# Three buffers instead of two for the gathered rows of a graph layer's first edge pass

## The chip, the core and the metric

The kernel runs on one core of a Trainium2 chip. The metric is device time in microseconds for one execution of the whole program, as the median of several runs.

## The reference, cut to what matters

The reference is four graph layers, each followed by a feed-forward layer, on 3125 nodes of 256 features and 50000 edges. The edges are sorted by destination. The change lies in the first graph layer, which sends two rounds of messages over the edges. Each edge has one of 16 relation types with a block-diagonal matrix of its own, and a weight:

```python
def _rel_graph_conv_bdd(x, src, dst, etype, norm, w, loop_w, bias):
    xs = x[src].reshape(e, nb, -1)
    we = w[etype]
    msg = jnp.einsum('ebi,ebio->ebo', xs, we)
    msg = msg.reshape(e, -1) * norm
    agg = jax.ops.segment_sum(msg, dst, num_segments=n)
    return agg + bias + x @ loop_w

h = jax.nn.relu(_rel_graph_conv_bdd(x, src, dst, etype, norm, w1, loop_w1, b1))
return _rel_graph_conv_bdd(h, src, dst, etype, norm, w2, loop_w2, b2)
```

Everything that follows (feed-forward layers with experts, attention over edges, a top-k graph layer) is not touched by the change.

## The kernel before, in words

Nodes are cut into 25 tiles of 125. The edges that end in one tile are laid out as T = 17 chunks of 128, one edge per partition. Before the first pass, the product of every node with every relation's matrix is written to a table in HBM, `rel_tab[0]`, with a row of 256 floats for each pair of node and relation.

A pass over the edges then goes through the tiles. For tile t, `front` makes two things. `one_hot` (L1255, on DVE) writes 17 masks `s` of 128 x 125: row by edge, the edge's weight in the column of its destination. `gathered` (L1233, on POOL) issues 17 indirect DMAs, one for each chunk, each of which fetches the 128 table rows that the chunk's edges name into a slice of the tile `g`. `edge_sums` (L1262, on PE) multiplies mask and rows chunk by chunk and adds all 17 products into one PSUM bank. Since the operands are 32-bit, each of the 17 products shows as two matmul records, with two weight loads.

`skewed` sets the order: `front(t)` is issued before `back(t - 1)`, so that a tile's gathers are issued one tile ahead of its sums. `g` and `s` come from pools with rotating buffers: with two of them, the gathers of tile t + 1 have to wait until the sums of tile t - 1 have read the buffer. POOL executes its gathers in order.

In the first pass, `back1` follows the sums of a tile with a good deal of other work: it adds `own_tab`'s row block and applies Relu (L1586, L1587), transposes the result (L1205), forms its products with all 16 relations for the second pass (`relation_rows`, L1495, evicted by DVE and ACT at L1046 and L1048), and writes them to `rel_tab[1]`, some 2 MB per tile, from SP's queue (L1055, L1056). It multiplies by the second loop matrix (L1594) and adds to `x` (L1596). Between these, `count` advances a generator that prepares counting tables for later layers (masks `kh` and `lh` on DVE at L1381 and L1383, matmuls at L1397 and L1411, evictions at L1401, L1414 and L1416). This is one instruction stream per engine, in the order in which it is written.

The second pass uses the same `front` with `layer` = 1 and reads `rel_tab[1]`, so it can gather only after the first pass has written all of it. Its sums are added to `x` at L1619; experts of the first feed-forward layer are woven into it.

Of the kernel before, what the change touches and what calls it, by code (L numbers as in the profile page):

```python
# [1022 lines left out]
def fast(ctx: ExitStack, tc: tile.TileContext, a: dict, out: bass.AP):  # L1023
# [14 lines left out]
    def bank():  # L1038
        return psum.tile([128, 512], F32, tag="ps", name="ps")
# [13 lines left out]
    def dma_rows(dst, src):  # L1053

        nc.sync.dma_start(dst[0:112], src[0:112])  # L1055
        return nc.sync.dma_start(dst[112:P], src[112:P])  # L1056
# [100 lines left out]
    def load_w(src, dst):  # L1157

        nc.sync.dma_start(dst, src.rearrange("(k p) m -> p k m", p=128))
        return dst  # L1160

    def load_row(src):

        n = src.shape[0]
        r = row_pool.tile([128, D], F32, tag="row", name="row")
        nc.sync.dma_start(r[:, :n], src.partition_broadcast(128))
        return r[:, :n]
# [9 lines left out]
    def over(row, n=NT):  # L1177
        return row[:P, None, :].to_broadcast([P, n, row.shape[1]])
# [21 lines left out]
    def transpose_tiles(src, dst, n):  # L1200

        for k in range(2):
            ps = bank()
            for i in range(n):
                nc.tensor.transpose(ps[:, i * P:(i + 1) * P], src[:, i, k * 128:(k + 1) * 128],  # L1205
                                    ident[:P, :P])
            evict(dst[:, k, :], ps[:, :n * P])
# [29 lines left out]
    def gathered(pool, table, idx, t, wide=0):  # L1237

        w = table.shape[1]
        g = pool.tile([128, T, max(w, wide)], F32, tag="g", name="g")  # L1240
        for k in range(T):
            gather(g[:, k, 0:w], table, idx, t * T + k)
        return g

    def one_hot(pool, t, w=None):


        s = pool.tile([128, T, P], F32, tag="s", name="s")
        for k in range(T):
            c = t * T + k  # L1250
            if w is None:
                nc.vector.tensor_scalar(s[:, k, :], iota, dst_l[:, c:c + 1], None,
                                        op0=ALU.is_equal)
            else:
                nc.vector.tensor_scalar(s[:, k, :], iota, dst_l[:, c:c + 1], w[:, c:c + 1],  # L1255
                                        op0=ALU.is_equal, op1=ALU.mult)
        return s

    def edge_sums(ps, s, g, w, start=True, stop=True):

        for k in range(T):
            nc.tensor.matmul(ps[:P, :w], s[:, k, :], g[:, k, 0:w],  # L1262
                             start=(start and k == 0), stop=(stop and k == T - 1))

    def skewed(front, back):

        held = front(0)
        for t in range(1, NT):
            nxt = front(t)
            back(t - 1, held)  # L1270
            held = nxt
        back(NT - 1, held)
# [187 lines left out]
    def relation_weights(pool, w):  # L1460


        mask = pool.tile([128, 128], F32, name="mask")
        half = pool.tile([128, 128], I32, name="half")
        halfp = pool.tile([128, 1], I32, name="halfp")
        halff = pool.tile([128, 1], F32, name="halff")
        nc.gpsimd.iota(half, pattern=[[1, 128]], base=0, channel_multiplier=0)
        nc.gpsimd.iota(halfp, pattern=[[0, 1]], base=0, channel_multiplier=1)
        nc.vector.tensor_scalar(half, half, 1, None, op0=ALU.arith_shift_right)
        nc.vector.tensor_scalar(halfp, halfp, 1, None, op0=ALU.arith_shift_right)  # L1470
        nc.vector.tensor_copy(halff, halfp)
        nc.vector.tensor_copy(mask, half)
        nc.vector.tensor_scalar(mask, mask, halff, None, op0=ALU.is_equal)
        wc = pool.tile([128, 2, R, 2], F32, tag="wc", name="wc")
        for k in range(2):
            nc.sync.dma_start(wc[:, k, :, :],
                              w[:, 64 * k:64 * (k + 1), :, :].rearrange("r b i o -> (b i) r o"))
        wbd = pool.tile([128, 2, R * 128], F32, tag="wbd", name="wbd")
        for k in range(2):
            nc.vector.tensor_mul(  # L1480
                wbd[:, k, :].rearrange("p (r j o) -> p r j o", r=R, o=2),
                wc[:, k, :, None, :].to_broadcast([128, R, 64, 2]),
                mask.rearrange("p (j o) -> p j o", o=2)[:, None, :, :]
                .to_broadcast([128, R, 64, 2]))
        return wbd
# [58 lines left out]
    def l0_gnn():  # L1544
        with ExitStack() as st:
            keys = st.enter_context(tc.tile_pool(name="l0", bufs=1)).tile(
                [128, 2, NT * NB], F32, name="keys")
            nc.sync.dma_start(keys, key_tab)
            cp = st.enter_context(tc.tile_pool(name="cnt0", bufs=2))
            work = counting(cp, keys)  # L1550
            ffn = None

            def count(n):
                for _ in range(n):
                    next(work, None)

            def front(layer, pools):
                hp = pools.enter_context(tc.tile_pool(name=f"hot{layer}", bufs=2))
                gp = pools.enter_context(tc.tile_pool(name=f"g{layer}", bufs=2))

                def f(t):
                    s = one_hot(hp, t, wgt)
                    g = gathered(gp, rel_tab[layer], rel_x, t)
                    return s, g
                return f

            with ExitStack() as s1:
                xp = s1.enter_context(tc.tile_pool(name="l0x", bufs=1))
                yp = s1.enter_context(tc.tile_pool(name="rely", bufs=2))
                tp = s1.enter_context(tc.tile_pool(name="h0", bufs=2))  # L1570
                ffn = SoftExperts(xp)
                loop = load_w(a["L0_gnn_loop_w2"], xp.tile([128, 2, D], F32, name="loop"))
                b2 = load_row(a["L0_gnn_b2"])
                wbd = relation_weights(xp, a["L0_gnn_w2"])
                for t0, n in GROUPS:
                    dma_rows(x[:, t0:t0 + n, :], x_view[:, t0:t0 + n, :])
                    nc.vector.tensor_add(x[:, t0:t0 + n, :], x[:, t0:t0 + n, :], over(b2, n))

                def back1(t, sg):
                    s, g = sg  # L1580
                    own = tp.tile([P, D], F32, tag="own", name="own")
                    dma_rows(own, own_tab[t * P:(t + 1) * P, :])
                    ps = bank()
                    edge_sums(ps, s, g, D)
                    h = tp.tile([P, 1, D], F32, tag="h", name="h")
                    nc.vector.tensor_add(h[:, 0, :], ps[:P, :D], own)  # L1586
                    nc.scalar.activation(h[:, 0, :], h[:, 0, :], AF.Relu)  # L1587
                    count(3)
                    ht = tp.tile([128, 2, P], F32, tag="ht", name="ht")
                    transpose_tiles(h, ht, 1)  # L1590
                    relation_rows(yp, rel_tab[1], ht, wbd, t, 0)
                    ps = bank()
                    for k in range(2):
                        nc.tensor.matmul(ps[:P, :D], ht[:, k, :], loop[:, k, :],  # L1594
                                         start=(k == 0), stop=(k == 1))
                    nc.vector.tensor_add(x[:, t, :], x[:, t, :], ps[:P, :D])  # L1596
                    count(4)

                skewed(front(0, s1), back1)

            ffn.load(st)
            queue = []

            groups = {1: (0, 2), 4: (2, 3)}
            groups.update({t0 + 3: (t0, 4) for t0 in range(5, NT, 4)})

            def feed(n):
                for _ in range(n):
                    while queue and next(queue[0], queue) is queue:
                        queue.pop(0)  # L1610

            def back2(t, sg):
                s, g = sg

                parts = 7 if t < 4 else 3
                count(parts)
                ps = bank()
                edge_sums(ps, s, g, D)
                nc.vector.tensor_add(x[:, t, :], x[:, t, :], ps[:P, :D])  # L1619
                count(parts)  # L1620
                feed(3)
                if t in groups:
                    queue.append(ffn.parts(*groups[t]))

            skewed(front(1, st), back2)
            count(1000)
            feed(1000)
# [1222 lines left out]
```

## Time and profile before

| what | value |
|---|---|
| median of 3 runs | 5268.94 us (5267.66 to 5290.92) |
| profiled execution | 5201.46 us, span 5199.8 us |
| PE busy over the span | 4044.8 us (78%) |
| DVE, ACT, POOL busy | 2545.4, 1434.1, 1522.9 us |
| first gather of the first pass | 299.15 us |
| last sum of the first pass | ends at 1035.18 us |
| first gather of the second pass | 1051.45 us |
| mean granted TensorE clock | 0.867 |

The first pass takes some 740 us, a seventh of the span; the change touches this stage. A row of a group of instructions gives, after the bar, the time in which the group was busy, the mean duration of one in ns, and the idle time of its engine just before them with what ended it. In a timeline, the first two numbers are start and length in us, and square brackets give the idle time before and what ended it. "Issue" stands where nothing that the profile shows ended the idle time; "remote" where it was a semaphore that nothing in the profile set at that time. PEld is the weight load of PE. POOL's records are the issue of a gather, not its transfer.

### The profile page before, as it was taken

The page shows a single profiled execution, that of the slowest core. Times are in us where ns is not written, and L with a number is a line of the kernel's source. Part 1 is how long each engine was busy: PE and PEld are TensorE (multiplying, and loading weights), DVE is VectorE, ACT ScalarE, POOL GpSimd, SP SyncE. Part 2 cuts the span into 40 slices and gives each one's busy share as a digit, 9 for nine tenths or more (in the row PEclk, how much of TensorE's full clock was granted, in tenths as well). Part 3 has the DMA queues.
Part 4 walks back from the last instruction along what each step waited for, and adds up shares of the span by engine and source line. Part 5 has one row for each costly group of instructions (what it writes and reads, how often), then busy time and mean ns, then how long its engine had stood idle before and what let it go on. Part 6 is the DMA issues. An engine that isn't in the chain of part 4 may idle for free.

```text
span 5199.8 us, 54230 instructions
## 1 busy us (share of the span) xinstructions
PE 4044.8 (78%) x18205; PEld 2954.4 (57%) x18205; DVE 2545.4 (49%) x8018; ACT 1434.1 (28%) x2894; POOL 1522.9 (29%) x1583
## 2 busy tenths in 40 slices
PE   6857777747888789999787989789983544449899
PEld 3434444535555555577675667678872433337766
DVE  4554444433333333311998682321113555559959
ACT  2212222222222222411335331123332222223452
POOL 1145555453443341000000100035533666620000
PEclk9978888868988899999898999879996766769999
DMA  8765555552222221022541014335544444434300
GB/s 218 224 183 188 175 185 173 176 171 78 79 69 70 70 81 43 19 79 73 146 115 33 15 25 133 108 112 172 172 147 116 116 114 112 114 104 127 103 7 26
DMA packets 208949, 581.19 MB, mean 112 GB/s; under 512 B 52941, under 2 KB 104583, under 8 KB 196099
## 3 DMA queue, kind: packets, MB, share of 16 engines
q1 hardware_dynamic: 115567, 327.42, 21.5%
q0 software_dynamic: 89456, 246.36, 16.0%
q10 hardware_dynamic: 3640, 3.85, 0.3%
q8 instruction: 148, 2.42, 0.2%
q14 instruction: 138, 1.13, 0.1%
HBM read 414.33 MB, written 167.02 MB: 112 GB/s over the span
## 4 chain that ended last, share of the span: by engine, by line
PE 52%; DVE 10%; issue 6%; DMA 3%; another core or an unknown queue 3%; ACT 3%; POOL 2%; DVEq 0%; SPq 0%; ACTq 0%
PE ps L1686 10%; PE ps L1228 7%; PE ps L2073 6%; PE ps L1441 5%; PE ps L2547 4%; PE ps L1942 4%; PE ps L2556 4%; PE ps L1262 3%; PE ps L1443 3%; POOL g L1233 2%; DVE pr L2069 2%; PE ps L2258 1%; DVE e L2065 1%; DMA row_tab<-hrow 1%
## 5 line engine op out<-in xcount | busy, mean ns | idle before, releaser
L1233 POOL DMA_INDIRECT g<-rel_tab,rel_x x850 | 815.4, 959 | 882.1 <-PE ps L1397 387.1
L1262 PE MATMUL ps<-g,s 128*125 128x256 f32 x1700 | 486.6, 434 | 168.1 <-issue 143.9
L2073 PE MATMUL ps<-hx,pr 125*125 125x257 f32 x2500 | 564.7, 384 | 51.8 <-DVE pr L2069 46.4
L2073 PEld LDWEIGHTS ps<-hx,pr 125*125 125x125 f32 x2500 | 462.0, 188 | 149.7 <-DVE pr L2069 76.1
L1262 PEld LDWEIGHTS ps<-g,s 128*125 128x125 f32 x1700 | 357.9, 215 | 276.6 <-issue 197.7
L1233 POOL DMA_INDIRECT g<-row_tab,src_x x425 | 420.9, 990 | 291.6 <-issue 155.7
L1942 PE MATMUL ps<-g,s 128*125 128x260 f32 (+1 forms) x850 | 249.5, 464 | 294.0 <-DVE g L1939 145.5
L1441 PE MATMUL ps<-xs,c_t 125*125 125x512 bf16 x1250 | 410.5, 380 | 6.7 <-DMA c_t<-c_tab 5.8
L1942 PEld LDWEIGHTS ps<-g,s 128*125 128x125 f32 x850 | 196.3, 235 | 341.0 <-issue 275.0
L1686 PE MATMUL ps<-xt,w 128*128 128x500 f32 (+2 forms) x896 | 372.8, 567 | 11.9 <-DMA w<-in_L_ffn_W_dram,rows 11.9
L1443 PE MATMUL ps<-xs,c_t 125*125 125x256 bf16 x1250 | 341.3, 273 | 0.2 <-DVE xs L1430 0.2
L2067 ACT ACTIVATE e<-e,e 125x375 f32<-125x375 f32 (+1 forms) x450 | 248.4, 584 | 311.7 <-DVE e L2065 254.8
L1228 PE MATMUL ps<-w,h 128*125 128x256 f32 x1200 | 285.7, 393 | 36.2 <-ACT h L1689 18.1
L1689 ACT ACTIVATE h<-ps,bn_b,bn_s 128x500 f32<-128x500 f32 (+2 forms) x224 | 159.6, 722 | 502.7 <-PE ps L1686 332.9
L1228 PEld LDWEIGHTS ps<-w,h 128*125 128x125 f32 x1200 | 232.2, 195 | 96.3 <-issue 30.2
L1686 PEld LDWEIGHTS ps<-xt,w 128*128 128x128 f32 x896 | 179.0, 203 | 176.7 <-issue 138.5
L1692 DVE SCALAR_TENSOR_TENSOR x<-ps,gate,x 125x256 f32<-125x256 f32 x200 | 94.1, 481 | 342.9 <-PE ps L1228 223.9
L2547 PE MATMUL ps<-xgt,w 128*128 128x128 f32 x1792 | 252.7, 285 | 3.5 <-ACT h L2549 2.0
L1381 DVE TENSOR_SCALAR kh<-iota_b,keys 128x125 bf16<-128x125 bf16 x625 | 162.7, 266 | 180.0 <-remote 73.7
L2547 PEld LDWEIGHTS ps<-xgt,w 128*128 128x128 f32 x1792 | 231.3, 195 | 28.6 <-ACT h L2549 12.2
L2065 DVE SCALAR_TENSOR_TENSOR e<-r,e 125x375 f32<-125x375 f32 (+1 forms) x450 | 244.7, 571 | 0.5
L1255 DVE TENSOR_SCALAR s<-iota,dst_l,wgt 128x125 f32<-128x125 f32 x850 | 241.2, 357 | 6.5 <-PE ps L1262 6.5
(463 smaller groups left out, 6536.0 us busy)
## 6 DMA issues: line engine op xcount, KB each, us to landing
rel_tab<-y SPq DMA_DIRECT2D x100, 896.0 KB
c_t<-c_tab SPq DMA_DIRECT2D x50, 683.6 KB
mk<-m_tab SPq DMA_DIRECT2D x50, 683.6 KB
c<-c_tab SPq DMA_DIRECT2D x50, 683.6 KB
c_tab<-c_t SPq DMA_DIRECT2D x25, 683.6 KB
m_tab<-m_t SPq DMA_DIRECT2D x25, 683.6 KB
g<-rel_tab,rel_x POOLq DMA_INDIRECT x850
st<-dst_tab SPq DMA_DIRECT2D x25, 476.0 KB
```

The lines of the kernel that those rows point to most:

```text
L1228: nc.tensor.matmul(ps[:P, :m], xt[:, k, t * P:(t + 1) * P], w[:, k, :], start=(k == 0), stop=(k == kk - 1))
L1233: nc.gpsimd.indirect_dma_start(out=dst, out_offset=None, in_=table, in_offset=bass.IndirectOffsetOnAxis(ap=idx[:, c:c + 1], axis=0))
L1255: nc.vector.tensor_scalar(s[:, k, :], iota, dst_l[:, c:c + 1], w[:, c:c + 1], op0=ALU.is_equal, op1=ALU.mult)
L1262: nc.tensor.matmul(ps[:P, :w], s[:, k, :], g[:, k, 0:w], start=(start and k == 0), stop=(stop and k == T - 1))
L1441: nc.tensor.matmul(pa[:P, :], c_t[:, s, :], xs[:, s, 0:2 * D], start=(s == 0), stop=last)
L1443: nc.tensor.matmul(pb[:P, :D], c_t[:, s, :], xs[:, s, 2 * D:3 * D], start=(s == 0), stop=last)
L1686: nc.tensor.matmul(ps[:, :n * P], w[:, k, fo * 128:(fo + 1) * 128], xt[:, k, t0 * P:(t0 + n) * P], start=(k == 0), stop=(k == kk - 1))
L1942: nc.tensor.matmul(ps[:P, :wide], s[:, k, :], g[:, k, 0:wide], start=(k == 0), stop=(k == T - 1))
L2065: nc.vector.scalar_tensor_tensor(e[:, :w], r[:, 0, :w], self.e8[:, s:s + 1], r[:, 1, :w], op0=ALU.add, op1=ALU.max)
L2067: nc.scalar.activation(e[:, :w], e[:, :w], AF.Exp, bias=self.e2[:, s:s + 1])
L2073: nc.tensor.matmul(ps[i][:P, :D + 1], pr[:, i, :], self.hx[:, s, 0:D + 1], start=(s == 0), stop=(s == NT - 1))
L2547: nc.tensor.matmul(o, w[:, k, fo * 128:(fo + 1) * 128], xt[:, k, :], start=(k == 0), stop=(k == 1))
```

## The change

The pool of gathered rows gets `3 - layer` buffers: three in the first pass, two as before in the second. The masks' pool keeps two in both.

```diff
             def front(layer, pools):
                 hp = pools.enter_context(tc.tile_pool(name=f"hot{layer}", bufs=2))
-                gp = pools.enter_context(tc.tile_pool(name=f"g{layer}", bufs=2))
+                gp = pools.enter_context(tc.tile_pool(name=f"g{layer}", bufs=3 - layer))
 
                 def f(t):
                     s = one_hot(hp, t, wgt)
```

The order in which everything is issued stays as it is. The gathers of tile t + 1 now wait for the sums of tile t - 2 instead of those of tile t - 1.

## The prediction

> **What bounds the kernel now.** I read the page first, to find the gathers and the matmuls that use them. Write burst t for the 17 gathers of node tile t (L1233 on POOL), M(t) for the 34 matmul records that sum that tile's edges (L1262 on PE), and e(t) for the end of M(t).
>
> ```profile
> L1233 POOL DMA_INDIRECT g<-rel_tab,rel_x x850 | 815.4, 959 | 882.1 <-PE ps L1397 387.1
> L1262 PE MATMUL ps<-g,s 128*125 128x256 f32 x1700 | 486.6, 434 | 168.1 <-issue 143.9
> ```
>
> Both passes are in these rows (850 gathers are 2 x 25 x 17). POOL sits idle before gathers until PE is done. L1397 is only the matmul that ends just after M(t); what frees the buffer is M(t). The PE row already says something else: its idle time is "issue", time in which it waited for nothing the profile shows, not for DMA.
>
> Next, the waits from 350 to 1050 us, which is the first pass without its start:
>
> ```profile
> PEld ps L1262 <- issue: 179.5, 152, 3.8
> PE ps L1262 <- issue: 135.2, 117, 3.6
> POOL g L1233 <- PE ps L1397: 153.8, 19, 11.0
> PE ps L1262 <- DMA g<-rel_tab,rel_x: 7.2, 6, 1.6
> ```
>
> POOL loses 153.8 us to the two buffers. PE loses 7.2 us waiting for gathered data and 135.2 us to "issue". A third buffer acts on the first number. The question is whether the second and third are connected to it.
>
> The POOL timeline gives the pace:
>
> ```profile
> 412.48 0.94 POOL L1233 DMA_INDIRECT g<-rel_tab,rel_x  x1 [8.41 <-PE ps L1397]
> ...
> 432.50 0.94 POOL L1233 DMA_INDIRECT g<-rel_tab,rel_x  x1 [0.30 <-issue]
> 440.61 0.95 POOL L1233 DMA_INDIRECT g<-rel_tab,rel_x  x1 [7.17 <-PE ps L1397]
> ...
> 460.64 0.95 POOL L1233 DMA_INDIRECT g<-rel_tab,rel_x  x1 [0.30 <-issue]
> 468.83 0.94 POOL L1233 DMA_INDIRECT g<-rel_tab,rel_x  x1 [7.24 <-PE ps L1397]
> ```
>
> A gather every 1.25 us, 21.0 us for a burst, then 7 to 8 us of waiting. Counting 17 at a time from the first gather at 299.15, these are bursts 4, 5 and the start of 6. Burst 5 begins when M(3) ends, as two buffers demand.
>
> The PE timeline of the same time:
>
> ```profile
> 450.82 4.28 PE L1262 MATMUL ps<-g,s 128*125 128x256 f32 x18
> 456.13 0.38 PE L1262 MATMUL ps<-g,s 128*125 128x256 f32 x1 [1.03 <-DMA g<-rel_tab,rel_x]
> 457.55 0.45 PE L1262 MATMUL ps<-g,s 128*125 128x256 f32 x1 [1.04 <-issue]
> ...
> 464.55 4.00 PE L1262 MATMUL ps<-g,s 128*125 128x256 f32 x9 [0.40 <-issue]
> ```
>
> This is M(4). Its own gathers were issued from 412.48 to 433.45; in the trace's packet records the last packet of burst 4 lands at 434.9, 16 us before M(4) starts. So it has all its data, runs 18 records, then crawls for 9 us and recovers about 3 us after the last gather of burst 5 was issued (461.6). The profile names a DMA once, but that data had landed at 428; the name is only the nearest one. The crawl goes with another tile's burst running on POOL. The last tile is the test, for no burst is left beside it:
>
> ```profile
> 1000.45 3.92 PE L1262 MATMUL ps<-g,s 128*125 128x256 f32 x17
> ...
> 1012.34 4.85 PE L1262 MATMUL ps<-g,s 128*125 128x256 f32 x14 [2.04 <-issue]
> ...
> 1027.62 7.56 PE L1262 MATMUL ps<-g,s 128*125 128x256 f32 x34
> 450.70:468.60 17.90, 12.03 (x34) 7.85 (x34) 0.74 0.44 145
> 1027.50:1035.30 7.80, 7.56 (x34) 6.32 (x34) 1.00 0.39 127
> ```
>
> M(23), beside burst 24, takes 16.7 us. M(24), with the same work and no burst, takes 7.56. The last two rows are windows of M(4) and M(24) (length, PE busy, PEld busy, granted clock, DMA share, GB/s): total DMA traffic is nearly equal, so the burst, not the load on the DMA engines, goes with the crawl; the clock falls to half only after the crawl began. Other engines crawl too:
>
> ```profile
> 374.14 0.42 DVE L1596 TENSOR_TENSOR x<-x,ps 125x256 f32<-125x256 f32 x1 [15.09 <-remote]
> 1097.89 0.42 DVE L1619 TENSOR_TENSOR x<-x,ps 125x256 f32<-125x256 f32 x1 [41.63 <-remote]
> ```
>
> The input of the first was ready at 346.5 (L1594); DVE goes on 2 us after bursts 0 to 2, which run back to back, end at 372.1. The second lies in pass 2, 4 us after bursts 25 and 26 end at 1093.7. In every tile from 2 to 23 PE executes 113 to 131 records from the start of a burst to the first crawl, whether that takes 13 or 19 us: it looks as if engines live off a stock of instructions while a burst runs. That is an inference; the working needs only the pattern.
>
> So the pass is a loop: e(t) starts a burst (21.0 us), M(t+1) cannot finish until 6.5 to 9.4 us after its last gather, and e(t+1) starts the next. From e(1) = 382.86 to e(23) = 1017.19 that is 22 periods of 28.83 us.
>
> **The change part by part.** It adds no instruction and removes none; the second pass keeps two buffers. It costs 17 x 256 x 4 bytes = 17 KB more of each partition. I cost this at nothing: whatever later uses that space waits at most for M(23), over 30 us before the second pass's first gather (1051.45). If that cover were gone, the price would be a part of the 16 us between e(24) and that gather.
>
> *Steady state.* Burst t+2 no longer waits for e(t) but for e(t-1), which is long past; the burst that now starts at e(t) is t+3. POOL needs 21.0 us per tile and PE's loop 28.8, so after a few tiles POOL has used up the third buffer and is again released by each e(t), at the same phase to PE. Nothing else runs on POOL here (425 instructions from 300 to 1040 us, all gathers), so nothing is queued behind its wait. Change per tile: 0. The masks keep two buffers on DVE; they cost DVE 6.5 us of waiting in the whole pass and stay hidden.
>
> *Start.* Bursts 0 to 2 now run without a wait from 299 to 372.1, and burst 3 waits 11.0 us until 383.13. With a third buffer burst 3 needs only e(0) = 334.3: it follows at 372.4 and ends at 393.3. M(1) has 18 of its 34 records left at 376.2, and recovers after 393.3 instead of 372.1. With a tail of 7.5 us (10.8 after burst 2 with 18 records left, fewer now), e(1) is 400.8 instead of 382.9: +17.9. Bounds: if PE gets through M(1) while burst 3 runs, burst 4 follows with no pause and e(2) is about 422 instead of 412.2, +9.9; with the tail of 10.8 it is +21.2. I take +17.9, by the nearest row, the crawl of 8 records in 19 us in M(1). Burst 4 then starts at e(1), and the loop runs as before.
>
> *End.* The last burst starts one period earlier, at e(21). M(22) is the last that crawls; M(23) runs like M(24). The step from e(22) to e(23) takes 18.0 us (as e(23) to e(24)) instead of 27.7: -9.7.
>
> *Sum.* +17.9 - 9.7 = +8.2 us, carried to the end, since the second pass starts after the last table rows of the first are written. On the profiled execution (5201.46, span 5199.8) that is 5209.7, up 0.16%. The three runs have a median of 5268.94, 1.3% above the profiled one; I add the same 8.2 to it: 5277.
>
> *A rule against this.* The POOL row above repeats the same wait of 7 to 8 us in each tile. The Trainium skill, "Perfetto Trace Analysis", section "Identifying Performance Opportunities", says that the same gap repeating on the engine that should be saturated can mean that there is too little SBUF for the next tile, that is, too few buffers. If POOL were that engine, its 7.6 us per tile over 22 tiles would be worth 167 us. The trace disagrees: the engine short of time is PE, which waits for gathers 7.2 us in 700. By the rule 5102, by the trace 5277.
>
> **The rivals.**
> *Faster.* If PE's crawl came from late data after all, bursts ahead would end it, and the pass would go at POOL's 21.25 us per tile (PE's own work is 18.0): 22 x (28.83 - 21.25) = 167 us less, 5102. For it: the releaser "DMA g" in some crawls, and the size of POOL's wait. Against it: landings 16 us ahead, and M(1), which crawls longest, 29.8 us, just where bursts run longest. 6%, a partial gain included.
>
> *Slower: the long burst at the start starves DVE as in pass 2.* Four bursts now run for 94 us. After bursts 25 and 26, the pause of 4.4 us was too short: burst 27 began at 1098.13 with DVE behind, and e(25) to e(26) took 57.2 us (1078.28 to 1135.46). If e(1) to e(2) takes that instead of 28.8, add 28.4: +36.6, 5305.5. For it: DVE has some 8 us of work queued from 395 on, and burst 4 starts at 401. Against it: a pause of 11 us was enough at 372, and 7.2 us is enough after every single burst. It decides from a delay of 36 us at the start (26 plus the 9.7 won back). 10%.
>
> *No effect*, the third buffer never in use: burst 3 would still wait until 383; 5269. Against it: e(0) is 38 us before burst 2 ends. It counts as no change.
>
> **How the numbers follow.** 0.5% is 26 us, about what a measurement of this kernel can tell from no change. Likeliest case and no effect together 84%: 5262 to 5292, from 0 to +11.5 at the start and the spread of 23 us among the three runs. Slower 10%, faster 6%. The range for 8 in 10 reaches some way to both: 5254 to 5302.
>
> **What would show it.** In the changed profile: burst 3 without a wait, ending near 393; e(1) near 401; then the same waits of 7 to 8 us before bursts from about burst 6 on, and a period of 28.8; M(23) at 7.6 us; the last gather of the pass near 1000 instead of 1010.7; second pass and the rest unchanged in length, shifted by some 8 us. The prediction is wrong if POOL's waits vanish for good with M(t) shorter than 15 us, or if the period itself moves by over 1 us.

## The result and the profile after

| | kernel before | changed kernel |
|---|---|---|
| median of the comparison, 20 runs each | 5274.74 us (5257.47 to 5290.92) | 5288.12 us (5279.06 to 5296.14) |
| profiled execution, span | 5201.46, 5199.8 us | 5280.89, 5279.2 us |
| first gather, e(0), e(1) | 299.15, 334.34, 382.86 us | 297.18, 332.03, 403.00 us |
| e(22), e(23), e(24) | 989.47, 1017.19, 1035.18 us | 1033.92, 1052.45, 1070.44 us |
| mean period from e(1) to e(22) | 28.89 us | 30.04 us |

The ratio is 1.0025, with a 95% interval from 1.0018 to 1.0033. On 5274.74 us that is 13.4 us slower (9.5 to 17.4): inside the 0.5% that was called no change, and a real loss none the less.

The profiled execution of before was quicker than all 20 timed runs of that kernel. So the two columns must not be subtracted over the whole pass; the first experiment below gives a pair from one chip for that. What each profile shows in itself can be read here. First, the page of the changed kernel:

```profile
L1233 POOL DMA_INDIRECT g<-rel_tab,rel_x x850 | 815.9, 960 | 953.7 <-PE ps L1397 432.1
L1262 PE MATMUL ps<-g,s 128*125 128x256 f32 x1700 | 499.3, 441 | 212.2 <-issue 182.6
```

Its longest waits from 350 to 1050 us (in all, how many, the longest):

```profile
PEld ps L1262 <- issue: 203.8, 145, 3.9
POOL g L1233 <- PE ps L1397: 184.4, 20, 11.3
PE ps L1262 <- issue: 154.7, 127, 3.6
```

POOL still loses more to waiting for a buffer than to anything else. With one more wait of 8.0 us that the profile puts under another name (L1411), these are 21 waits, one for each burst from 4 to 24. A third buffer did not take that wait away. Now POOL's timeline at the start of the pass:

```profile
371.06 0.95 POOL L1233 DMA_INDIRECT g<-rel_tab,rel_x  x1 [0.30 <-issue]
...
391.07 0.95 POOL L1233 DMA_INDIRECT g<-rel_tab,rel_x  x1 [0.30 <-issue]
403.27 0.94 POOL L1233 DMA_INDIRECT g<-rel_tab,rel_x  x1 [11.26 <-PE ps L1397]
433.33 0.94 POOL L1233 DMA_INDIRECT g<-rel_tab,rel_x  x1 [9.09 <-PE ps L1397]
```

The first two lines are the first and last gather of burst 3: it no longer waits, and four bursts run in one stretch. Burst 4 then waits 11.26 us, for M(1), and from there the loop of burst and wait runs as before. The PE timeline shows M(1) and the two last tiles:

```profile
345.37 1.99 PE L1262 MATMUL ps<-g,s 128*125 128x256 f32 x8 [1.75 <-issue]
...
373.48 0.59 PE L1262 MATMUL ps<-g,s 128*125 128x256 f32 x1 [1.52 <-issue]
376.98 0.59 PE L1262 MATMUL ps<-g,s 128*125 128x256 f32 x1 [2.91 <-issue]
...
400.08 2.92 PE L1262 MATMUL ps<-g,s 128*125 128x256 f32 x6 [0.82 <-issue]
1044.90 7.55 PE L1262 MATMUL ps<-g,s 128*125 128x256 f32 x34
1062.88 7.56 PE L1262 MATMUL ps<-g,s 128*125 128x256 f32 x34
474.00:492.80 18.80, 11.47 (x44) 8.05 (x43) 1.16 (x6) 3.10 (x6) 8.41 (x9) 0.73 0.44 138
1044.80:1052.50 7.70, 7.70 (x39) 6.49 (x37) 4.04 (x26) 1.53 (x4) 0.00 (x0) 1.00 0.37 119
```

M(1) crawls, one record every two to three us, until 400 us: 8 us after burst 3 has ended. It takes 57.6 us. M(23), beside the last burst in the kernel before, now runs alone and takes 7.55 us. The last two rows are windows of M(4), which crawls beside burst 6, and of M(23) (length, PE, PEld, DVE, ACT and POOL busy, granted clock, DMA share, GB/s): POOL is busy for 8.41 us in the first and not at all in the second, and the traffic is much the same.

### The profile page after: what moved, and what is told of

The parts are those of the page before. It is cut to its first block, busy times and chain, and to the rows that moved or that the text cites. A ratio compares the mean times of both kernels' runs of the same rounds, so it can differ in the third digit from the quotient of the medians.

```text
span 5279.2 us, 54229 instructions
## 1 busy us (share of the span) xinstructions
PE 4069.8 (77%) x18205; PEld 2964.2 (56%) x18205; DVE 2550.4 (48%) x8018; ACT 1432.7 (27%) x2894; POOL 1519.7 (29%) x1583
## 4 chain that ended last, share of the span: by engine, by line
PE 57%; issue 11%; DVE 10%; POOL 8%; DMA 6%; another core or an unknown queue 5%; ACT 3%; SPq 0%; POOLq 0%; DVEq 0%; ACTq 0%
PE ps L1686 9%; POOL g L1233 7%; PE ps L1262 7%; PE ps L1228 7%; PE ps L2073 6%; PE ps L1441 5%; PE ps L2547 4%; PE ps L2556 4%; PE ps L1942 4%; PE ps L1443 3%; PE ps L1495 2%; PE ps L2258 2%; DVE pr L2069 2%; DVE e L2065 1%
## 5 line engine op out<-in xcount | busy, mean ns | idle before, releaser
L1262 PE MATMUL ps<-g,s 128*125 128x256 f32 x1700 | 499.3, 441 | 212.2 <-issue 182.6
```

Source lines behind the costliest of these rows:

```text
L1262: nc.tensor.matmul(ps[:P, :w], s[:, k, :], g[:, k, 0:w], start=(start and k == 0), stop=(stop and k == T - 1))
```

## The experiments

Time of each run, with the kernel before on the same chip beside it:

| run | chip | kernel before | this run | ratio (95%) |
|---|---|---|---|---|
| base: the kernel before | 1 | 5261.29 | 5264.16, one run | |
| three: the changed kernel | 1 | 5261.29 | 5278.8, one run | |
| plain | 1 | 5261.29 | 5192.91 | 0.9881 (0.9854 to 0.9909) |
| pause2 | 1 | 5261.29 | 5273.53 | 1.0030 (1.0019 to 1.0041) |
| held3 | 14 | 4688.06 | 4688.45 | 0.9997 (0.9987 to 1.0006) |
| late3 | 14 | 4688.06 | 4693.19 | 1.0008 (0.9997 to 1.0019) |
| stop2 | 14 | 4688.06 | 4792.9 | 1.0231 (1.0212 to 1.0251) |
| stop3 | 14 | 4688.06 | 4800.02 | 1.0231 (1.0214 to 1.0249) |
| three_b: the changed kernel | 2 | 4689.91 | 4689.49 | 0.9997 (0.9989 to 1.0005) |
| held3_b | 2 | 4689.91 | 4694.22 | 1.0005 (0.9997 to 1.0014) |
| stop2_b | 2 | 4689.91 | 4802.0 | 1.0236 (1.0219 to 1.0253) |
| holdstop | 3 | 5271.45 | 5231.78 | 0.9927 (0.9899 to 0.9955) |

The column of the kernel before holds a surprise: chips 14 and 2 run the same program 11% quicker than chips 1 and 3. The result above was measured on the slow kind, by its time. Times are compared on one chip only; where traces of two chips stand side by side below, the text says so.

### base and three: a pair on one chip

No edit; both kernels as they are.

> The kernel before, profiled on the same chip as the next runs. Open is why the period from e(1) to e(22) is 28.9 us in the profile of before and 30.0 in that of the changed kernel. If the third buffer does not touch the loop and the profiled execution of before was merely a quick one (5201 us, the 20 timed runs 5257 to 5291), the period here is near 30 us and e(24) comes some 760 to 768 us after the first gather. If the third buffer itself slows the loop, the period is 28.9 here again and e(24) comes 736 us after the first gather.

> The changed kernel on the same chip. The prediction's account: bursts 0 to 3 back to back, e(1) 17 to 21 us later than in the kernel before on this chip, M(23) at 7.6 us, and between them the same period within 0.3 us. If the third buffer slows the loop, the period is longer than before's on this chip by about 1 us, 21 us in the pass.

POOL's timeline of base and then of three, where it first waits; and the last two tiles on PE, again base first:

```profile
390.03 0.94 POOL L1233 DMA_INDIRECT g<-rel_tab,rel_x  x1 [12.97 <-PE ps L1397]
```

```profile
410.44 0.95 POOL L1233 DMA_INDIRECT g<-rel_tab,rel_x  x1 [13.48 <-PE ps L1397]
```

```profile
1023.44 3.65 PE L1262 MATMUL ps<-g,s 128*125 128x256 f32 x15
...
1035.87 5.99 PE L1262 MATMUL ps<-g,s 128*125 128x256 f32 x15 [1.54 <-issue]
1052.29 7.56 PE L1262 MATMUL ps<-g,s 128*125 128x256 f32 x34
```

```profile
1039.24 7.55 PE L1262 MATMUL ps<-g,s 128*125 128x256 f32 x34
1057.22 7.55 PE L1262 MATMUL ps<-g,s 128*125 128x256 f32 x34
```

| stretch of the first pass | base | three | difference |
|---|---|---|---|
| first gather to e(0) | 34.25 us | 36.92 us | +2.7 |
| e(0) to e(1) | 51.51 | 71.81 | +20.3 |
| e(1) to e(22), 21 periods | 622.43 (29.64 each) | 618.09 (29.43 each) | -4.3 |
| e(22) to e(23) | 29.66 | 18.54 | -11.1 |
| e(23) to e(24) | 17.99 | 17.98 | 0.0 |
| sum | 755.84 | 763.34 | +7.5 |

The signs that the prediction named are there: a loss at the start, a smaller gain at the end, and a loop that keeps its pace. The first row is none of them: it ends before burst 3, the first that the third buffer lets start sooner, so its 2.7 us only show how far two executions differ. The pass of base is a little shorter than the 760 to 768 us expected of it; its period of 29.64 us is near the 30 us. The first wait ends 109.0 us after the first gather instead of 86.0 (410.44 - 301.44, and 390.03 - 304.00): the 2.7 and the 20.3 us of the first two rows.

### plain: the same bytes without POOL

The first pass fetches its rows by plain DMAs from SP, of the same size and number, from other rows of the table, so its sums are other sums.

```diff
-                    g = gathered(gp, rel_tab[layer], rel_x, t)
+                    if layer:
+                        return s, gathered(gp, rel_tab[layer], rel_x, t)
+                    g = gp.tile([128, T, D], F32, tag="g", name="g")
+                    for k in range(T):
+                        r0 = 100 * (t * T + k)
+                        nc.sync.dma_start(g[:, k, :], rel_tab[0][r0:r0 + 128, :])
```

> Two buffers. In the first pass the rows come by 17 plain DMAs per tile of the same size, 128 table rows in a row, issued by SP; POOL issues none there. The rows are then not those that the edges name, so the sums are other sums; the work of PE, DVE and ACT is the same. If the crawl comes from POOL's issuing of gathers, M(t) takes 7.6 us in all tiles, the period falls towards 18 to 21 us, and the time falls by 170 to 250 us. If it comes from the traffic into SBUF, M(t) stays at 16 us or more and the time within 40 us of before.

A line of plain's PE timeline, M(5), and its window; then the window from 400 to 950 us, of base and of plain:

```profile
460.40 7.55 PE L1262 MATMUL ps<-g,s 128*125 128x256 f32 x34
460.40:468.00 7.60, 7.60 (x38) 6.36 (x36) 3.76 (x25) 1.43 (x3) 0.00 (x0) 1.00 0.86 266
```

```profile
400.00:950.00 550.00, 398.59 (x1493) 253.01 (x1491) 231.47 (x950) 122.69 (x238) 298.06 (x315) 0.82 0.55 175
```

```profile
400.00:950.00 550.00, 411.50 (x1632) 263.33 (x1631) 257.89 (x1053) 135.31 (x262) 0.00 (x0) 0.81 0.61 190
```

From tile 4 to tile 22 every M(t) takes 7.55 us (base: 13.5 to 19.9), although the DMA engines move more: 190 GB/s against 175, and 266 GB/s during M(5) itself, where the crawling M(4) of the prediction had 145. So it is POOL's gathers that go with the crawl, not the amount of traffic. plain changes two things at once, though: which engine issues, and that each fetch reads 128 rows that lie in a row. No run gathers scattered rows from another queue, so the issuing and the gather's own kind of transfer are not told apart by it. The time falls by 1.2%, about 63 us (48 to 77), and not by the 170 to 250 us expected, since a new wait took over:

```profile
PE ps L1205 <- ACT h L1592: 131.1, 20, 7.7
SPq L1055 <- DVE y L1046: 202.9, 42, 8.4
```

In these waits from 400 to 950 us, PE waits 6.6 us per tile for the result that L1205 transposes, and SP's queue, which now holds the fetches as well, waits for each tile's table rows before it goes on. The mean period from e(1) to e(22) is 26.8 us, against 29.6 in base.

### pause2: idle work on POOL, in no fixed order

```diff
+                    for k in range(T):
+                        if k == 9:
+                            for _ in range(4):
+                                nc.gpsimd.iota(idle, pattern=[[1, 700]], base=0,
+                                               channel_multiplier=0)
+                        gather(g[:, k, :], rel_tab[0], rel_x, t * T + k)
```

> Two buffers. After the ninth gather of each burst of the first pass POOL fills a scratch tile four times (about 5 us) before the other eight; nothing else changes. If a burst starves the other engines and a pause of over 3 us lets them restock, M(t) stops crawling, and the period becomes POOL's own, about 26.5 us, 2 to 3.5 us less than before: 50 to 80 us faster. If a pause does not restock, each burst is 5 us longer, the loop too, and it is about 110 us slower.

The iotas did not stay in the middle of the bursts. POOL's timeline shows single ones inside burst 1, then 15 in a row ahead of burst 2, and the last five ahead of burst 8:

```profile
349.05 0.74 POOL L1573 IOTA idle<- 128x700 int32 x1
...
361.61 11.79 POOL L1573 IOTA idle<- 128x700 int32 x15
...
556.66 3.86 POOL L1573 IOTA idle<- 128x700 int32 x5
610.54 0.95 POOL L1233 DMA_INDIRECT g<-rel_tab,rel_x  x1 [7.55 <-PE ps L1397]
```

As a test of a stop inside each burst it is void, and its time (+0.3%) settles nothing. Two of its tiles are of use. With the single iotas in burst 1 and a break of 11.79 us behind it, the step from e(0) to e(1) is 24.1 us instead of 51.5. And where the iotas are used up, bursts 8 (560.7 to 581.7) and 9 (582.0 to 603.0) run back to back; M(8), beside them, takes 38.1 us, and the step to e(8) 50.5 us where the same kernel's neighbours take 32.4 and 30.4. So two bursts in a row cost about 20 us in the middle of the pass too, with two buffers; M(8)'s own rows were still being gathered for its first 9.5 us, so not all of its 38.1 us is the crawl.

### held3 and late3: the third buffer without its early burst

In held3 the pass has three buffers, but the rows of each tile's 17th chunk go to a pool of their own with two, and are gathered first; so a burst can begin no earlier than with two buffers. In late3 the same holds for the first 21 tiles only.

```diff
+                    ep = pools.enter_context(tc.tile_pool(name="end", bufs=2))
...
+                    g = gp.tile([128, T, D], F32, tag="g", name="g")
+                    end = ep.tile([128, D], F32, tag="end", name="end")
...
+                        ins = gather(end, rel_tab[0], rel_x, t * T + T - 1)
+                        order.enter_context(tc.issue_after(ins.ins))
+                        for k in range(T - 1):
+                            ins = gather(g[:, k, :], rel_tab[0], rel_x, t * T + k)
```

> Three buffers as in the change, but the last chunk's rows lie in a pool of two buffers and are gathered first in each burst, so that POOL waits as with two buffers. This leaves the place and size of the third buffer and undoes its effect on the order. If the time of the change comes from the back-to-back bursts at the start and the burst less at the end, this kernel is within 0.1% of before, with e(1) as before. If the third buffer's place in memory costs something, it is as slow as the change, 0.2 to 0.3%.

> As held3 up to tile 20; from tile 21 on the third buffer is free to be used, so the lead is taken late: burst 21 follows burst 20 at once. If two bursts back to back cost some 20 us wherever they are, M(19) crawls through both and ends about 20 us late, M(23) runs in 7.6 us, and the whole is 8 to 14 us slower than before, like the change. If the cost belongs to the start of the pass alone, only the 11 us at the end remain and it is 8 to 11 us faster than before.

They ran on a chip of the quick kind, and say nothing about the start and the end: in both, POOL's gathers of the first pass run from 300.4 to 843.7 us (held3) and from 306.1 to 848.2 us (late3) with no wait for a buffer over 0.3 us, the mean period is 21.4 us, and both times are those of the kernel before. The burst-then-wait loop is not there on every chip.

### stop2 and stop3: a stop inside every burst

Three iotas between the 9th and the 10th gather of all 25 bursts, burst 0 too, in a fixed order, with two buffers (stop2) or three (stop3):

```diff
+                            if k in (9,):
+                                for _ in range(3):
+                                    order.enter_context(tc.issue_after(ins.ins))
+                                    ins = nc.gpsimd.iota(idle, pattern=[[1, 1600]], base=0,
+                                                         channel_multiplier=0)
+                                order.enter_context(tc.issue_after(ins.ins))
+                            ins = gather(g[:, k, :], rel_tab[0], rel_x, t * T + k)
```

> Two buffers; from burst 1 on POOL fills a scratch tile three times, about 5 us, between the ninth and the tenth gather of each burst of the first pass, now with its place in POOL's order fixed. If a pause lets the engines restock, M(t) no longer crawls to the end, the loop is set by POOL's 26 us per tile, and it is 50 to 80 us faster than before. If the crawl ends only after a whole burst, each loop is 5 us longer and it is about 110 us slower.

> The same pause with three buffers. If the pause lets the engines restock, PE no longer needs POOL to stop between bursts, POOL runs ahead without harm, and the period is POOL's 26 us, as with two buffers or up to 10 us less in all. If it does not, it is about 110 us slower than before, and the start is slower still by some 20 us.

On this chip POOL is the bound of the pass, and neither run can tell the two expectations apart. The gap between the two gathers grows from 0.3 to 4.7 us, the period from 21.4 us (held3) to 25.7 (stop2) and 25.5 us (stop3), and 25 x 4.4 = 110 us is what the times show (+105 and +112).

### three_b, held3_b and stop2_b: another chip

The same three kernels again; in the expectation for held3_b, what is called the last chunk is each tile's 17th chunk.

> The changed kernel again. Two kinds of chip have shown so far: in one the kernel before takes about 5265 us, and engines stop while a burst of 17 gathers is issued; in the other it takes about 4688 us and the 850 gathers run back to back. Where the burst-then-wait loop is there, both theories of the change (start +18 to +20 us, end -10 to -11 us) give +8 to +17 us. Where the gathers run back to back, POOL never waits for a buffer, so the third buffer is never taken into use earlier than the second would be: within 0.1% of before. A clear loss there would mean that the third buffer costs something besides the start of the loop.

> Three buffers, but the rows of the last chunk (tiles 24 and on of the pass, two of them, gathered ahead of the rest from a pool of their own) are what the early issue is spent on, so that the loop itself never has a third burst waiting. Where the burst-then-wait loop is there: within 0.2% of before by the theory that the loss is one more burst at the start. By the rival, that the loss comes from where the buffers lie or from the later passes, +8 to +17 us as in the changed kernel. Where the gathers run back to back: within 0.1% of before by both.

> Two buffers, and POOL does three iotas of about 4 to 5 us in all between the 9th and the 10th gather of every burst, in a fixed order. Where the burst-then-wait loop is there: by the theory that the other engines run dry during a burst and are supplied again when POOL stops issuing gathers, the stop lets them work on, the period falls from about 29 to about 26 us, and the kernel is 50 to 80 us faster. By the rival, that only the end of a burst frees them, each tile takes 4 to 5 us more: 100 to 115 us slower. Where the gathers run back to back POOL is the bound and the stop adds itself: about 105 us slower by both.

This was again a chip of the quick kind, and now the changed kernel has a profile there. POOL's timeline at the two ends of burst 5 (the last gather of burst 4, the first and last of burst 5, the first of burst 6), and the window from 350 to 840 us, of base on chip 1 and of three_b on chip 2:

```profile
415.79 0.95 POOL L1233 DMA_INDIRECT g<-rel_tab,rel_x  x1 [0.30 <-issue]
417.04 0.94 POOL L1233 DMA_INDIRECT g<-rel_tab,rel_x  x1 [0.30 <-PE ps L1262]
...
437.21 0.95 POOL L1233 DMA_INDIRECT g<-rel_tab,rel_x  x1 [0.30 <-issue]
438.47 0.95 POOL L1233 DMA_INDIRECT g<-rel_tab,rel_x  x1 [0.30 <-issue]
```

```profile
350.00:840.00 490.00, 345.47 (x1278) 218.94 (x1278) 204.53 (x839) 107.02 (x209) 266.56 (x282) 0.81 0.54 172
```

```profile
350.00:840.00 490.00, 431.91 (x1876) 281.86 (x1876) 289.29 (x1193) 152.11 (x299) 371.12 (x391) 0.96 0.76 245
```

The gathers run without a break across the border of two bursts. That holds for the 425 gathers of the first pass and not, as the expectation has it, for all 850: in the second pass POOL waits on this chip too (from 1036.1 to 1047.3 us, for one). In the same 490 us the quick chip executes 1876 records on PE against 1278, with 391 gathers against 282 and 245 GB/s against 172. From M(1) on, M(t) takes 7.6 to 12.0 us, with gathers running beside it. It now runs while its own burst is still being issued (M(4) from 408.8 us, burst 4 until 416.7), so what it waits for is data that is really still to land:

```profile
PE ps L1262 <- DMA g<-rel_tab,rel_x: 28.8, 29, 2.5
```

Two buffers are enough here: in the whole pass each e(t) comes 16 to 19 us before burst t + 2 starts (e(1) at 356.0, burst 3 at 374.4; e(4) at 419.3, burst 6 at 438.5), so the third buffer changes nothing, and the ratio is 0.9997. The stop costs 2.36%, on chip 14 2.31%. No trace of the kernel before was kept on a chip of the quick kind.

### holdstop: both questions in one kernel

held3's arrangement, and stop2's iotas in the bursts of tiles 12 to 24 only:

```diff
                         for k in range(T - 1):
+                            if k == 8 and t >= 12:
+                                for _ in range(3):
+                                    order.enter_context(tc.issue_after(ins.ins))
+                                    ins = nc.gpsimd.iota(idle, pattern=[[1, 1600]], base=0,
+                                                         channel_multiplier=0)
+                                order.enter_context(tc.issue_after(ins.ins))
                             ins = gather(g[:, k, :], rel_tab[0], rel_x, t * T + k)
```

> Three buffers, with the 17th chunk's rows of every tile in a pool of their own with two buffers and gathered first, so that a burst can start no earlier than with two; and, in tiles 12 to 24 of the first pass only, three iotas (4 to 5 us in all) between the 9th and the 10th gather of each burst. Both are to be read in the trace by tile. Where the burst-then-wait loop is there (kernel before near 5265 us): by the theory of the prediction the step from e(0) to e(1) is again about 51 us and the one from e(22) to e(23) 27 to 30 us, as with two buffers; if the start's loss comes from the third buffer's place and not from the early burst, e(0) to e(1) stays at 71 us. In tiles 12 to 23 the period falls from about 29 to about 26 us if POOL's stop lets the other engines go on (in all some 35 us faster), and rises to about 33 us if only the end of a burst does (some 55 us slower). Where the gathers run back to back (kernel before near 4689 us): POOL is the bound, the stop adds 4 to 5 us to each of 13 bursts, some 55 us slower, and the two buffers of the 17th chunk cost nothing.

This one ran on a chip of the slow kind, and answers both. *The start and the end.* From e(0) to e(1) it takes 49.7 us: as with two buffers (51.5 in base on chip 1), not as with three (71.8), though all three buffers are there. At the end M(23) again lies beside burst 24 and takes 17.3 us, so the end's gain is gone too; the step from e(22) to e(23), 28.9 us, says less, since the steps among the tiles with the stop vary from 18.0 to 36.0 us. The start's loss belongs to the early burst, not to where the buffers lie, and so in all likelihood does the end's gain.

*The stop.* POOL's timeline of burst 12 and PE's timeline of M(12), M(14) and M(16), M(12) beside burst 13 and so on (two of the 34 records now read the 17th chunk's tile):

```profile
666.07 0.95 POOL L1233 DMA_INDIRECT g<-rel_tab,rel_x  x1 [0.30 <-issue]
667.03 4.55 POOL L1584 IOTA idle<- 128x1600 int32 x3
671.73 0.97 POOL L1233 DMA_INDIRECT g<-rel_tab,rel_x  x1 [0.15 <-issue]
```

```profile
696.09 7.12 PE L1611 MATMUL ps<-g,s 128*125 128x256 f32 x32
703.05 0.59 PE L1611 MATMUL ps<-end,s 128*125 128x256 f32 x2
...
748.20 7.12 PE L1611 MATMUL ps<-g,s 128*125 128x256 f32 x32
...
805.15 7.12 PE L1611 MATMUL ps<-g,s 128*125 128x256 f32 x32
```

The crawl is gone from most tiles: of the twelve M(t) from 12 to 23, ten take 7.6 to 9.8 us and two over 17 us, where base has 14.6 to 19.9. The mean period from e(10) to e(23) is 26.7 us. In the same trace, without the stop, it is 29.8 us from e(1) to e(10), so the gain is not the chip's, nor that of the 17th chunk's pool or of the fixed order, which all tiles have; base has 29.5 and 29.7 us in the two stretches. The windows from 655 to 1000 us, of base on chip 1 and then of holdstop on chip 3:

```profile
655.00:1000.00 345.00, 256.00 (x957) 160.97 (x956) 152.94 (x626) 77.81 (x152) 189.63 (x201) 0.82 0.56 179
```

```profile
655.00:1000.00 345.00, 256.42 (x1044) 168.64 (x1043) 180.61 (x689) 85.78 (x169) 262.21 (x254) 0.85 0.61 194
```

POOL has 4.4 us more to do per tile, and everything gets done sooner: 1044 records on PE in place of 957. The first gather to e(24) takes 725.9 us against 755.8 in base; on chip 3 the time falls by 0.73%, or 39 us (24 to 53), against the kernel before there. It was not run beside the changed kernel there, nor on a chip of the quick kind, where stop2 and stop3 lose 2.3% by the same stop in 25 tiles.

## Why the prediction was right, point by point

**What bounds the pass.** Right, for chips of the slow kind. The crawl is set by POOL's gathers and not by late data or by the load on the DMA engines: plain takes the gathers away and leaves the bytes, and M(t) falls to 7.55 us; holdstop interrupts the issuing for 4.7 us, and it falls to 7.6 to 9.8 us in ten tiles of twelve. So the length of an unbroken stretch of gathers counts: broken in the middle, it mostly does not bring PE to its crawl. What the engines run out of stays open. The prediction inferred a stock of instructions, and the trace gives that no support. The records of the instruction queues, with 0.9 to 1.4 us for a 16 KB packet, look alike in base and in three_b. And in base no packet of these queues moves between 573.4 and 599.6 us, while M(8) begins at 577.9, crawls from 580.9 and ends at 596.2: no load of instructions ends that crawl.

**Steady state, 0 per tile.** Right: 29.43 against 29.64 us in the pair of one chip, with the waits back from burst 4 on, mostly 7 to 9 us each after that burst's. By the text's own test, a period that moves by over 1 us, the first two profiles would have refuted it (30.04 against 28.89). The pair shows that this was the quick execution of before, not the third buffer.

**Start, +17.9.** Right in kind: burst 3 ended at 392.0 us, 393.3 was foretold. The pair shows +20.3. The mis-sized term is the tail. The text let M(1) end 7.5 us after burst 3; it ended 11.0 us after it in the first profile and 13.2 us after it in the pair (410.2 - 397.0). The prediction had the 10.8 us of burst 2 at hand, which gave its upper bound of +21.2, and took less because fewer records are left. But the tail did not shrink: after three bursts it was 10.8 us (before) and 12.7 us (base), after four 11.0 and 13.2 us. Fewer records were left, but the crawl outlasted the longer stretch by more: by 2.4 us after the single burst 24 and 5.8 us after bursts 0 to 2 in base, by 8.6 us after bursts 0 to 3 in three (to the start of the last unbroken run of records of M(23), M(1) and M(1)).

**End, -9.7.** Right: -11.1 in the pair. The new step, 18.5 us, was foretold as 18.0; the old one was 29.66 us in that execution, and 27.7 us in the one that the prediction worked from.

**Sum, +8.2.** The pass is 7.5 us longer in the pair. That this is so near is in part luck: the loss at the start was forecast 2.4 us too small and the gain at the end 1.4 us, which nearly cancel (20.3 - 11.1 = 9.2), and the rest of the sum, +2.7 and -4.3, is difference between two executions. The second pass keeps its length, as foretold: 1041.0 and 1041.6 us from its first gather to e(49), its last sum.

The whole kernel loses 13.4 us (9.5 to 17.4), more than the forecast sum, and where the rest lies is open. From e(49) to the end of the span, both profiles of the changed kernel are longer than their partners, by 7.2 us (3147.6 and 3140.4) and by 9.1 us (3154.4 and 3145.3). But two kernels with two buffers, on the same chip as the pair, differ as much there (3145.1 us in pause2 and 3155.1 us in plain), so this does not point to the third buffer; and three_b loses nothing on its chip.

**The rivals.** The slower one fell: e(1) to e(2) takes 30.1 us after the four bursts, and 29.0 in the pair, not 57.2. The faster one described another chip. On chips 14 and 2 the pass does go at POOL's pace, 21.3 to 21.4 us per tile, with M(t) held up by data that lands as it is needed. But there two buffers already allow it, and the third brings nothing. So the rule of the Trainium skill ("Perfetto Trace Analysis", "Identifying Performance Opportunities"), that the same gap repeating on the engine that should be saturated can mean too few buffers, has no engine to apply to on either kind: on one, POOL's gap is the echo of PE's crawl, and PE is the engine short of time; on the other, there is no gap.

## What to carry to other kernels

Before adding a buffer, ask whether the engine that waits for it is the one the stage is short of. If it is not, the loop settles at the old pace after a few turns, and what remains is one extra turn at the start and one fewer at the end; here they cost 20 us and gave back 11. Where an engine's long stretch of issuing slows the others, look for a break in the stretch, not for a longer one, and measure it on more than one chip: the same break of 4.7 us gained 0.7% on one kind, in 13 tiles, and lost 2.3% on the other, in 25.

## What was not expected of the hardware

The same program takes about 5265 us on some chips and 4689 us on others, and it is the gathering passes that differ: first gather to e(24) 755.8 us in base and 546.6 us in three_b, whose third buffer made no difference there; from the second pass's first gather to e(49) 1041.0 and 767.9 us. Of the 584 us between these two spans, 482 lie there. The mean granted clock goes along (0.863 and 0.908), as it does with PE's pace within one trace: 0.73 in the window of the crawling M(4) of the changed kernel, 1.00 in that of its M(23). Whether the cause is the chip or something about it at that time was not separated.

On the slow kind, a burst of 17 gathers stalls PE and DVE with everything at hand, and M(t) needs 13.5 to 19.9 us from M(2) to M(23) in base; with the same gathers running without a break on the quick kind, it needs 7.6 to 12.0 us from M(1) on in three_b.
